# An intermediate image in HBM without zeros between its rows, and a norm factor that is zero where a shifted column has no source

## The chip, the cores and the metric

The kernel runs on one core of one Trainium2 chip. The metric is the device time in microseconds of one execution. Engines are called as the profile calls them: PE is the matmul engine (PEld its weight loads), DVE the vector engine, ACT the scalar engine, POOL the GpSimd engine, and SP the engine that issues almost all of the DMAs. Each engine runs its own list of instructions in order, and so does SP's queue of DMAs: what stands behind a waiting instruction waits too.

## The reference, cut to what matters

The input x has 32 images of 192 channels of 56 x 56 pixels. Four layers follow one another, each of the form x = x + layer(norm(x)), with a group norm over 32 groups of six channels:

```python
x = x + attention(_gn(x))          # layer 0
x = x + wkv_scan(_gn(x))           # layer 1, forwards and backwards
x = x + shift_and_smooth(_gn(x))   # layer 2
x = x + long_filter(_gn(x))        # layer 3, an FFT convolution per channel
```

The change lies around layer 2. Its 192 channels form 48 positions of four channels each; a position has an offset (dx, dy). The image of a channel is moved by the rounded offset, pixels without a source become zero, and a 3 x 3 Gaussian, whose middle is the rest of the offset, smooths what comes out:

```python
out = x[:, :, y - Ry, x - Rx] * mask      # R = round(offset), mask = source inside the image
kern = exp(-((f + delta_x)**2 + (f + delta_y)**2) / (2 * 0.5**2)); kern /= kern.sum()
out = depthwise_conv(out, kern, padding=1)
```

## The kernel before, in words

The program has four stages in a row.

`make_filter` (L250) computes layer 3's filter and its spectra: sines of a small network in chunks (`sine`, L292 to L319), a decay and a product (L324 to L337), and row and column transforms (L350 to L369). Before it computes, it issues its loads and, by `beside()`, those of attention's constants and first image (`_Ready.load`, L397). `_find_shifts` (L208), called at L282 ahead of the sines, loads the 48 offsets (L215) and computes on DVE, with one exponential on ACT, what layer 2 needs of them: the taps along x, the taps along y, the rounded dy, and in `begins` where in a row each position's read begins. Both go to HBM (L244, L247).

`attention` (L408) works image by image and writes x1 to HBM. At the end of each image, SP stores the image and its statistics (L860 to L867), and then six channels' worth of zeros (L868 to L874): x2 in HBM is laid out by channel, parity s of the image, row h (57 rows, the last one holds the mean), image pair g, and then PITCH = 112 numbers, of which the first 56 are the row and the other 56 are zeros (`gaps`, L1807 to L1810). A row read from a position shifted by up to 56 columns to either side so finds zeros where its source lies outside the image. The zeros are written from one SBUF tile, 399 KB per channel, 192 times. The order behind the last store of the image is fixed by a dependency (L873 to L874).

`scan_pairs` (L907) takes two images at a time, and `finish` (L1201) writes their rows into x2 (L1253). Its first loads (L936 to L942) stand in SP's queue behind the last image's stores.

`channel_blocks` (L1518) does layers 2 and 3 channel by channel for all 32 images at once: two images lie in 114 partitions (57 rows each), 16 pairs along the free dimension. Six channels form a group, which is also the norm's group. `prepare(c)` (L1599) is called four channels ahead. It reads the channel's image at the shifted place (L1618), 16 pieces of 56 numbers a partition, into one of three `shifted` tiles, which have a zero column at either side; POOL multiplies by the norm's factor (L1619); ACT and POOL sum the three taps along x (L1622 to L1626). `matrix(n)` (L1562) builds, once per position, the matrix of the taps along y on POOL (L1567 to L1572) and PE (L1574). `shift` (L1630) loads the channel unshifted (L1635), multiplies by that matrix (L1641) and adds (L1642). `middle`, `centre` and `spread` make layer 3's norm (L1655 to L1670). `analyse` (L1672) transforms rows (L1787) and columns (L1683) and multiplies by the filter's spectra on DVE (L1690 to L1696), `synthesise` (L1699) transforms back (L1709, L1728), adds (L1729) and stores (L1732). While the second half of one group is normed, the group before is analysed and synthesised; the main loop (L1745 to L1769) writes down one order of steps.

That order isn't the one that runs. A planner takes the instructions in program order as their priority, estimates when each will be ready, and lays down each engine's list from that; an instruction from later in the program can so stand before one from earlier. Buffers are handed out from pools of fixed counts: 15 tiles for x, eight `padded`, three `shifted`.

Of the kernel before, what the change touches and what calls it, by code (L numbers as in the profile page):

```python
# [20 lines left out]
F32 = mybir.dt.float32  # L21
I32 = mybir.dt.int32
# [6 lines left out]
C = 192  # L29
T = 96  # L30
S = 56
# [36 lines left out]

PITCH = 2 * S
# [3 lines left out]
def _resize_matrix():  # L73
# [9 lines left out]
    (114, (114,)), (114, (114,)), (114, (1,)),  # L83
# [3 lines left out]
def _constants():  # L87
# [16 lines left out]
    for t in range(2):  # L104
# [17 lines left out]
        "chan_k": _filled([f[n] for n in "f1 f2 f3 f4 ones_rows ones_u lags diff_y at_rows".split()]),  # L122
# [3 lines left out]
def _spectral_constants():  # L126
# [21 lines left out]
    for s in range(2):  # L148
# [15 lines left out]
        "diff_y": diff_y,  # L164
        "at_rows": row[:, None],
# [42 lines left out]
def _find_shifts(nc, cp, a, k, taps, begins):  # L208
# [4 lines left out]
    found = cp.tile([PR, NP, 9], F32, name="found", tag="found")  # L213
# [28 lines left out]
    for f in range(3):  # L242
        nc.vector.tensor_scalar(found[:, :, 6 + f], rnd[:, :, 1], float(1 - f), None, ALU.add)
    nc.sync.dma_start(out=taps, in_=found)  # L244
    first = cp.tile([1, NP], I32, name="first", tag="first")
# [5 lines left out]
def make_filter(ctx: ExitStack, tc: tile.TileContext, a, consts, filt, spectra, shifts, beside):  # L251
# [30 lines left out]
    _find_shifts(nc, cp, a, consts, *shifts)  # L282
# [40 lines left out]
    tc.add_manual_dep(loaded.ins, last.ins.name, behind, reason="the sines' set")  # L323
    for t in range(2):  # L324
# [83 lines left out]
def attention(ctx: ExitStack, tc: tile.TileContext, a, ready, x1, st_a, st_c, x2, gaps):  # L408

# [48 lines left out]
    zeros = cp.tile([2 * (S + 1), LEAD], F32, name="zeros", tag="zeros")  # L458
    for t in (*agents_b[0], *agents_b[1], v_a, v_c, zeros):
        nc.gpsimd.memset(t, 0.0)  # L460
    for at in (0, x2.shape[0] - LEAD):
        nc.sync.dma_start(out=x2[at : at + LEAD].unsqueeze(0), in_=zeros[0:1])
# [343 lines left out]
    for b in range(NB):  # L806
# [57 lines left out]
        for h, r in HALVES:  # L864
            stored = nc.sync.dma_start(
                out=x1[b, 128:C, 1568 * h : 1568 * h + 1568], in_=x[1][r].rearrange("p y x -> p (y x)")
            )  # L867
        for c in range(C * b // NB, C * (b + 1) // NB):  # L868
            laid = nc.sync.dma_start(
                out=gaps[c].rearrange("s h g w -> (s h) g w"),  # L870
                in_=zeros[:, 0:S].unsqueeze(1).to_broadcast([2 * (S + 1), NB // 2, S]),
            )
            behind = mybir.DependencyInfo(mybir.DependencyClass.NoSync, mybir.DependencyReason.DATA)  # L873
            tc.add_manual_dep(laid.ins, stored.ins.name, behind, reason="no burst")  # L874
# [643 lines left out]
def channel_blocks(ctx: ExitStack, tc: tile.TileContext, shifts, k, flat_x2, x2, rs2, spectra, out):  # L1518
# [12 lines left out]
    xp = ctx.enter_context(tc.tile_pool(name="d_x", bufs=15))  # L1531
# [5 lines left out]
    found = cp.tile([PR, NP, 9], F32, name="found", tag="found")  # L1537
# [11 lines left out]
    f1, f2, f3, f4, ones, ones_u, lags, diff_y, _ = pieces  # L1549
    eps = cp.tile([PR, 1], F32, name="eps", tag="eps")  # L1550
    nc.vector.memset(eps, GN_EPS)
    padded = [cp.tile([PR, NI, 64], F32, name=f"padded{i}", tag=f"padded{i}") for i in range(8)]
# [3 lines left out]
    shifted = [cp.tile([PR, NI, S + 2], F32, name=f"shifted{i}", tag=f"shifted{i}") for i in range(3)]  # L1556
# [5 lines left out]
    def matrix(n):  # L1562

        if n not in made:
            t = [wp.tile([PR, PR], F32, name=f"tap{f}", tag=f"tap{f}", bufs=1) for f in range(3)]
            for f in range(3):
                nc.gpsimd.tensor_scalar(  # L1567
                    t[f], diff_y, found[:, n, 6 + f : 7 + f], found[:, n, 3 + f : 4 + f], ALU.is_equal, ALU.mult
                )
            mat = wp.tile([PR, PR], F32, name="mat", tag="mat", bufs=3)  # L1570
            nc.gpsimd.tensor_tensor(t[0], t[0], t[1], ALU.add)
            nc.gpsimd.tensor_tensor(mat, t[0], t[2], ALU.add)  # L1572
# [24 lines left out]
    SPAN = PR * NI * PITCH  # L1597

    def prepare(c):  # L1599
# [12 lines left out]
        if c % 4 == 0:  # L1612
            begin_at[i] = nc.values_load(
                begins[0:1, i : i + 1], engines=(mybir.EngineType.SP,), min_val=LEAD - S, max_val=LEAD + S
            )
        t = shifted[c % len(shifted)]
        there = flat_x2[bass.ds(begin_at[i] + c * SPAN, SPAN)].rearrange("(p g w) -> p g w", p=PR, w=PITCH)
# [312 lines left out]
```

## Time and profile before

| what | value |
|---|---|
| runs | 12225.82, 12207.08, 12215.15 us; median 12215.15 us |
| the profiled execution | 12216.98 us, span 12215.1 us, mean granted PE clock 0.958 |
| filter, to 163 us | PE 91.0 us busy, DVE 78.6 |
| attention, 163 to about 4920 us | PE and DVE busy over 80% |
| scan, about 4920 to 8435 us | DVE busy 3013 of the 3100 us from 5200 to 8300 |
| channels, about 8435 us to the end | from 8700 to 12000: PE 3163, DVE 2953, ACT 2088, POOL 1249 of 3300 us |
| HBM | 482.13 MB read, 319.29 MB written |
| DMA packets | 1959211, of which 1821153 are under 512 bytes |

A line of a timeline gives the start, the time from the first to the last of the instructions merged in it, the engine, the line of the program, the operation, its output and inputs, and how many there were; in brackets is the idle time of the engine before it and what ended that. A line of the groups gives the count, the busy time in all and the mean of one in ns, and behind the second bar the idle time before them.

### The profile page before, as it was taken

The page shows a single profiled execution, that of the slowest core. Times are in us where ns is not written, and L with a number is a line of the kernel's source. Part 1 is how long each engine was busy: PE and PEld are TensorE (multiplying, and loading weights), DVE is VectorE, ACT ScalarE, POOL GpSimd, SP SyncE. Part 2 cuts the span into 40 slices and gives each one's busy share as a digit, 9 for nine tenths or more (in the row PEclk, how much of TensorE's full clock was granted, in tenths as well). Part 3 has the DMA queues.
Part 4 walks back from the last instruction along what each step waited for, and adds up shares of the span by engine and source line. Part 5 has one row for each costly group of instructions (what it writes and reads, how often), then busy time and mean ns, then how long its engine had stood idle before and what let it go on. Part 6 is the DMA issues. An engine that isn't in the chain of part 4 may idle for free. (4 is left out here: it accounts for less than half of the span.)

```text
span 12215.1 us, 157485 instructions
## 1 busy us (share of the span) xinstructions
PE 11030.6 (90%) x57358; PEld 6623.6 (54%) x57358; DVE 10753.1 (88%) x14722; ACT 7146.9 (59%) x14690; POOL 3400.5 (28%) x2568
## 2 busy tenths in 40 slices
PE   6999999999999999688888888886999999999999
PEld 3555555555555555333333333333666666666666
DVE  6888888888888888799999999996888899898897
ACT  3555555555555555466666666665666666666665
POOL 0000000000000000455555555555343343343330
PEclk9999999999999999899999999997999999999999
DMA  2222222222222222243334334334333333333331
GB/s 70 57 57 57 59 58 64 59 59 59 63 61 57 57 57 49 73 103 96 97 101 104 93 97 104 98 96 100 71 68 64 67 70 64 67 70 64 67 69 32
DMA packets 1959211, 876.56 MB, mean 72 GB/s; under 512 B 1821153, under 2 KB 1858292, under 8 KB 1949292
## 3 DMA queue, kind: packets, MB, share of 16 engines
q1 hardware_dynamic: 1948188, 840.69, 30.1%
q10 hardware_dynamic: 10240, 25.70, 0.8%
q8 instruction: 458, 7.50, 0.3%
q14 instruction: 325, 2.66, 0.1%
HBM read 482.13 MB, written 319.29 MB: 66 GB/s over the span
## 5 line engine op out<-in xcount | busy, mean ns | idle before, releaser
L619 DVE SCALAR_TENSOR_TENSOR o<-v_a,att_w,o 128x896 f32<-128x896 f32 (+1 forms) x1024 | 1056.8, 1032 | 467.3 <-ACT v_a L593 337.3
L1142 POOL MEMSET f<- 128x1 f32 x96 | 8.9, 99 | 4769.6 <-DMA st_c<-st 4764.6
L1793 ACT COPY y<-ps 64x252 f32<-64x252 f32 (+1 forms) x2376 | 808.7, 340 | 797.3 <-PE ps L1787 767.6
L1626 POOL TENSOR_TENSOR smooth<-smooth,more 114x896 f32<-114x896 f32 x384 | 866.3, 2259 | 1200.7 <-ACT more L1625 1141.2
L1709 PE MATMUL ps<-fixed,real 84*84 84x112 f32 x6144 | 1093.6, 260 | 0.0
L1709 PE MATMUL ps<-fixed,imag 84*84 84x112 f32 x6144 | 1091.1, 259 | 0.0
L1717 ACT ACTIVATE z<-ps,rs 84x112 f32<-84x112 f32 x3072 | 816.7, 355 | 322.1 <-PE ps L1709 319.5
L1709 PEld LDWEIGHTS ps<-fixed,real 84*84 84x84 f32 x6144 | 790.2, 154 | 158.4 <-issue 129.4
L1135 ACT ACTIVATE q<-q 128x784 f32<-128x784 f32 x384 | 328.5, 855 | 812.4 <-DVE q L1130 641.2
L1709 PEld LDWEIGHTS ps<-fixed,imag 84*84 84x84 f32 x6144 | 765.8, 153 | 0.0
L890 PE MATMUL ps<-sq,fixed 128*128 128x392 f32 x512 | 298.9, 746 | 425.9 <-ACT sq L1213 425.9
L636 ACT ACTIVATE pr<-ps,low 98x896 f32<-98x896 f32 (+1 forms) x384 | 352.3, 918 | 559.9 <-DVE low L634 559.9
L724 PE MATMUL ps<-gq_a,xs_a 128*112 128x294 f32 x1792 | 619.1, 427 | 45.7 <-DVE pq L729 45.7
L1787 PE MATMUL ps<-fixed,padded 114*128 114x168 f32 x3072 | 527.6, 322 | 134.6 <-DVE x L1729 118.3
L619 DVE SCALAR_TENSOR_TENSOR o<-v_c,att_w,o 128x448 f32<-128x448 f32 (+1 forms) x1024 | 638.3, 623 | 6.0 <-ACT v_c L604 0.9
L632 PE MATMUL ps<-xs_a,gk_a 128*98 128x448 f32 (+1 forms) x1536 | 637.1, 495 | 0.0
L633 PE MATMUL ps<-xs_c,gk_c 125*98 125x448 f32 (+1 forms) x1536 | 631.6, 492 | 0.0
L1728 PE MATMUL ps<-z,fixed 84*114 84x448 f32 x1536 | 609.7, 539 | 0.4 <-ACT z L1717 0.4
L725 PE MATMUL ps<-gq_c,xs_c 125*112 125x294 f32 x1792 | 608.3, 421 | 0.0
L890 PE MATMUL ps<-x,weights 128*128 128x392 f32 x1536 | 574.0, 517 | 31.1 <-DVE bv L1164 14.2
L737 ACT ACTIVATE pq<-pq 112x1176 f32<-112x1176 f32 x224 | 265.4, 1185 | 553.0 <-DVE pq L729 430.1
L1787 PEld LDWEIGHTS ps<-fixed,padded 114*128 114x128 f32 x3072 | 473.6, 198 | 206.1 <-DVE x L1729 140.5
(372 smaller groups left out, 29249.8 us busy)
## 6 DMA issues: line engine op xcount, KB each, us to landing
x<-x SPq DMA_DIRECT2D x576, 392.0 KB
x<-x SPq DMA_DIRECT2D x512, 196.0 KB
x<-zeros SPq DMA_DIRECT2D x192, 399.0 KB
shifted<-x SPq DMA_DIRECT2D x192, 399.0 KB
x<-x SPq DMA_DIRECT2D x192, 399.0 KB
out_x<-x SPq DMA_DIRECT2D x384, 196.0 KB
x<-in_x SPq DMA_DIRECT2D x32, 1568.0 KB
x<-x SPq DMA_DIRECT2D x32, 1568.0 KB
```

Of the source, the lines that this page charges most:

```text
L619: nc.vector.scalar_tensor_tensor(dst, tap(i), dww[:, t, i : i + 1], dst, ALU.mult, ALU.add)
L632: mm(ps[P2, h, :n], g[:, cols], xs_a[j][:, px], start=True, stop=False)
L633: mm(ps[P2, h, :n], gk_c[0:KC, 2 * j + h, cols], xs_c[j][0:KC, px], start=False, stop=True)
L724: mm(ps[:SUB, i, :HA], xs_a[j][:, px], g, start=True, stop=False)
L725: mm(ps[:SUB, i, :HA], xs_c[j][0:KC, px], gq_c[0:KC, 2 * j + (q + i) // ns], start=False, stop=True)
L890: mm(out, aa, srcs[t][h], start=True, stop=False)
L1626: nc.gpsimd.tensor_tensor(y, y, more, ALU.add)
L1709: nc.tensor.matmul(ps[:84, i * 2 * S : (i + 1) * 2 * S], part[:, i0 + i].rearrange("p s u -> p (s u)"), f3[:, m, :], start=(m == 0), stop= ...
L1717: nc.scalar.activation(z[:, i0 + i].rearrange("p m w -> p (m w)"), ps[:84, i * 2 * S : (i + 1) * 2 * S], AF.Copy, scale=q.rs[:, i0 + i : i ...
L1728: nc.tensor.matmul(got, f4[:, m, :], z[:, i0 : i0 + n, m, :], start=(m == 0), stop=(m == 1))
L1787: nc.tensor.matmul(ps[:, g * 168 : (g + 1) * 168], flat[:, (g0 + g) * 128 : (g0 + g + 1) * 128], f1, start=True, stop=True)
L1793: nc.scalar.copy(y[64 * m : 64 * m + 64, 2 * g0 + i : 2 * (g0 + n) : 2], got[64 * i : 64 * i + 64, :, :, m, :])
```

## The change

Rows of x2 now follow each other without gaps, PITCH is gone, and nothing writes zeros between them; two stores of 64 zeros, ahead of the first and behind the last row, move from attention into `_find_shifts`. The shifted read takes 896 numbers in one piece a partition, into a tile of its own (`took`, two buffers). At columns without a source this reads the end of the neighbouring row. The norm's factor is therefore made a tile of the full size, the factor times a row that is 1 where the column has a source and 0 elsewhere; it is made on POOL by two comparisons and two products once per position and group of norm (64 times in all), and POOL's product per channel is that of `took` and this tile, into one of now two `shifted` tiles. `found` carries two more numbers per position for the comparisons, and a constant holds the columns' numbers.

Beside this, `_find_shifts` is called after the sines instead of before them; the matrices of positions 0 and 1 are built on DVE; for channels 0, 2 and 4 DVE multiplies and adds the second and third tap in one instruction each, in place of ACT's product and POOL's sum; x has 14 buffers instead of 15, `padded` seven instead of eight.

```diff
@@ _find_shifts
+    for f in range(2):
+        nc.vector.tensor_scalar(found[:, :, 9 + f], rnd[:, :, 0], f * S - 0.5, None, ALU.add)
     nc.sync.dma_start(out=taps, in_=found)
+    zeros = cp.tile([1, LEAD], F32, name="zeros", tag="zeros")
+    nc.vector.memset(zeros, 0.0)
+    for at in (0, x2.shape[0] - LEAD):
+        nc.sync.dma_start(out=x2[at : at + LEAD].unsqueeze(0), in_=zeros)
@@ make_filter
     beside()
-    _find_shifts(nc, cp, a, consts, *shifts)
...
     tc.add_manual_dep(loaded.ins, last.ins.name, behind, reason="the sines' set")
+    _find_shifts(nc, cp, a, consts, *shifts)
@@ attention
-        for c in range(C * b // NB, C * (b + 1) // NB):
-            laid = nc.sync.dma_start(
-                out=gaps[c].rearrange("s h g w -> (s h) g w"),
-                in_=zeros[:, 0:S].unsqueeze(1).to_broadcast([2 * (S + 1), NB // 2, S]),
-            )
...
@@ channel_blocks
-    xp = ctx.enter_context(tc.tile_pool(name="d_x", bufs=15))
+    xp = ctx.enter_context(tc.tile_pool(name="d_x", bufs=14))
...
-    padded = [cp.tile([PR, NI, 64], F32, name=f"padded{i}", tag=f"padded{i}") for i in range(8)]
+    padded = [cp.tile([PR, NI, 64], F32, name=f"padded{i}", tag=f"padded{i}") for i in range(7)]
...
-    shifted = [cp.tile([PR, NI, S + 2], F32, name=f"shifted{i}", tag=f"shifted{i}") for i in range(3)]
+    shifted = [cp.tile([PR, NI, S + 2], F32, name=f"shifted{i}", tag=f"shifted{i}") for i in range(2)]
@@ matrix
+            engine = nc.vector if n < 2 else nc.gpsimd
...
-            nc.gpsimd.tensor_tensor(t[0], t[0], t[1], ALU.add)
-            nc.gpsimd.tensor_tensor(mat, t[0], t[2], ALU.add)
+            engine.tensor_tensor(t[0], t[0], t[1], ALU.add)
+            engine.tensor_tensor(mat, t[0], t[2], ALU.add)
@@ prepare
+        if (n, i) not in factors:
+            here, low = (wp.tile([PR, S], F32, name=m, tag=m) for m in ("here", "low"))
+            nc.gpsimd.tensor_scalar(here, at_cols, found[:, i, 9:10], None, ALU.is_gt)
+            nc.gpsimd.tensor_scalar(low, at_cols, found[:, i, 10:11], None, ALU.is_lt)
+            nc.gpsimd.tensor_tensor(here, here, low, ALU.mult)
+            factor = wp.tile([PR, NI, S], F32, name="factor", tag="factor")
+            nc.gpsimd.tensor_tensor(
+                factor, _bc(scales[n][:, j], [PR, NI, S]), here.unsqueeze(1).to_broadcast([PR, NI, S]), ALU.mult
+            )
...
+        took = wp.tile([PR, NI, S], F32, name="took", tag="took")
+        there = flat_x2[bass.ds(begin_at[i] + c * SPAN, SPAN)].rearrange("(p g w) -> p g w", p=PR, w=S)
+        nc.sync.dma_start(out=took, in_=there)
         t = shifted[c % len(shifted)]
-        there = flat_x2[bass.ds(begin_at[i] + c * SPAN, SPAN)].rearrange("(p g w) -> p g w", p=PR, w=PITCH)
-        nc.sync.dma_start(out=t[:, :, 1 : S + 1], in_=there[:, :, 0:S])
-        nc.gpsimd.tensor_tensor(t, t, _bc(scales[n][:, j], [PR, NI, S + 2]), ALU.mult)
+        nc.gpsimd.tensor_tensor(t[:, :, 1 : S + 1], took, factors[n, i], ALU.mult)
...
         for f in (1, 2):
+            if c < GROUP and c % 2 == 0:
+                nc.vector.scalar_tensor_tensor(y, t[:, :, f : f + S], taps[f], y, ALU.mult, ALU.add)
+                continue
             more = wp.tile([PR, NI, S], F32, name="more", tag="spare", bufs=3)
             nc.scalar.activation(more, t[:, :, f : f + S], AF.Copy, scale=taps[f])
             nc.gpsimd.tensor_tensor(y, y, more, ALU.add)
```

## The prediction

> **What bounds the kernel now.** I read the busy shares and slices first, then the windows by stage, then the waits and the chain around each seam that the edit touches.
>
> ```profile
> PE 11030.6 (90%) x57358; PEld 6623.6 (54%) x57358; DVE 10753.1 (88%) x14722; ACT 7146.9 (59%) x14690; POOL 3400.5 (28%) x2568
> ...
> PE   6999999999999999688888888886999999999999
> DVE  6888888888888888799999999996888899898897
> POOL 0000000000000000455555555555343343343330
> ```
>
> Four stages: filter (to 163 us), attention (to 4920), scan (to 8435), channels (to the end). No engine waits for a DMA inside attention, and in the scan ACT waits 15.1 us in all for x. The edit's places are three seams and the channel stage. The first seam, attention to scan, is SP's queue by time (start, us):
>
> ```profile
> 4926.92 1.23 SPq L865 DMA_DIRECT2D x<-x  x2
> 4928.19 30.03 SPq L869 DMA_DIRECT2D x<-zeros  x6
> 4958.33 5.58 SPq L936 DMA_DIRECT2D passing<-in_scan_o  x1
> 4963.96 0.42 SPq L936 DMA_DIRECT2D passing<-in_scan_c  x1
> ```
>
> The scan's first weights queue behind the last image's six zero stores; the waits give PE 44.3 us idle there, on "DMA x<-zeros". Nothing else runs.
>
> The second seam is inside the filter, DVE by time; the third, POOL at the entry to the channels:
>
> ```profile
> 56.82 0.21 DVE L218 TENSOR_SCALAR off<-off 114x96 f32<-114x96 f32 x1 [19.07 <-DMA off<-in_L_conv_offset]
> ```
> ```profile
> 8458.03 1.74 POOL L1619 TENSOR_TENSOR shifted<-shifted,scale 114x928 f32<-114x928 f32 x1
> ...
> 8475.54 8.42 POOL L1626 TENSOR_TENSOR smooth<-smooth,more 114x896 f32<-114x896 f32 x4
> ```
>
> The chain runs through POOL from 8450 to 8581. In the steady part the groups of lines from 8700 to 12000 are what I price with (mean ns of one, then idle before):
>
> ```profile
> L1626 POOL TENSOR_TENSOR smooth<-smooth,more 114x896 f32<-114x896 f32 x344 | 779.1, 2268 | 1152.2 <-ACT more L1625 1107.3 <-ACT smooth L1622 31.8
> L1619 POOL TENSOR_TENSOR shifted<-shifted,scale 114x928 f32<-114x928 f32 x170 | 310.4, 1826 | 443.9 <-DMA shifted<-x 443.8
> L1567 POOL TENSOR_SCALAR tap<-fixed,found 114x114 f32<-114x114 f32 x116 | 119.0, 1031 | 6.8
> ```
>
> Last, windows from one group's mean (L1657) to the next: length, PE, PEld, DVE, ACT, POOL busy, granted clock:
>
> ```profile
> 10104.10:10220.77 116.67, 111.85 (x653) 78.80 (x653) 103.85 (x154) 73.22 (x196) 46.57 (x28) 0.97 0.31 66
> 10220.77:10334.41 113.64, 108.34 (x651) 76.64 (x651) 102.91 (x152) 72.19 (x194) 41.53 (x23) 1.00 0.31 67
> 11940.91:12054.66 113.75, 110.16 (x651) 78.47 (x651) 99.89 (x153) 66.91 (x189) 26.84 (x12) 0.97 0.18 38
> ```
>
> PE is busy 94 to 96% of a group, DVE about 90%: PE sets the pace, DVE is close behind it. The 27 groups from 8607 to 11710 have a mean of 114.9 us: 14 with one tap matrix 114.1 (POOL 41.8), 13 with two 115.8 (POOL 46.6).
>
> **The change part by part.** The sum is against the profiled execution's 12216.98 us (span 12215.1); the median of the runs, 12215.15, lies 1.8 lower.
>
> *Zero stores gone (192 of 399 KB).* The last six take 30.03 us of SP's queue with every engine idle. The first load behind them takes 5.58 us to issue where its neighbour takes 0.42, so the seam gives 30.0 to 35.2 us. Late next are the weights' landing and the st_a round trip, which moved behind too. I take **-33**, between the ends, as x1's last store is still in flight at 4928. The other 186 stores lie in attention, where SP itself waits 2358 us for ACT at L566 and no engine waits for a DMA: nothing. Were SP late there, 30 us an image would already show as a wait.
>
> *x2 without gaps.* The scan writes as many 224-byte pieces, 224 bytes apart instead of 448: nothing, under DVE's 97% there; were the stores slower, ACT's 15.1 us of waiting for x might double (+15). In the channels two reads a channel become 114 long pieces instead of 1824. In steady flow only POOL waits for one: 129 waits, 444 us. The read took 6.08 us in the chain at 9253.8. Long pieces have one near row: found and fixed (800 KB) issued at 8444.6 and read at 8450.3. So 399 KB takes from 3 us (half of it) to 6.1 (no better).
>
> *One buffer fewer* of x, padded, shifted. A load of x goes out one channel (19 us) later; nobody waits for x now, and it is used four or more steps after its buffer frees. The sixth padded waits for PE's L1787 of the fifth instead of the fourth channel of the group before, a step (19 us) earlier than it: nothing. Without that cover, some 2 us of DVE a group (+60). The read goes to its own tile, so SP's L1618 no longer waits for ACT (532 us), only for POOL's product two channels back; out_x stores are queued behind it and gain.
>
> *_find_shifts later.* DVE stands 19.07 us at L218 for a 43 KB load that SP issues after the loads of attention. In program order its 22 DVE instructions now follow the sines; its loads keep their place in SP's queue. But the planner places by readiness: L326 and L332, from after the sines, already run between them (11.21, 17.50), and L218 sits in a gap of the sines. A lower priority moves it by one instruction while its load is thought to come when it did. Two new TENSOR_SCALARs and a memset (0.2 us each) and two zero stores, which move to SP's queue here from the start of attention, have slack behind taps. Bounds -19 and +1; I take **0**.
>
> *Entry to the channels.* POOL loses matrices 0 and 1 (each 3 x 0.757 + 2 x 0.426 = 3.1) and six adds of channels 0, 2, 4 (6 x 2.08): 18.7 us. It gains, up to channel 5, two factors of 3.1 (two TENSOR_SCALARs of 114x56 at half of 0.757 and a little, a small product at 0.3, a large one at 2.07) and six products at 2.08 instead of 1.74 (two full inputs, as L1626): 8.2 us. DVE, idle over 80% there, takes the adds at 1.15 (L619's form at 128x896) and the matrices. So channel 5, at which group 0 closes (8510), comes 10.5 us earlier. But group 1 needs channels 6 to 11, with another 8.2 added and nothing removed: -2.3 by the sum alone. Of POOL's 28 us of idling from 8444 to 8580, 14.2 are waits for ACT's products, half of which go with DVE's adds. Ends -25 and 0; I take **-12**.
>
> *Steady part.* POOL per group of six: products 6 x (2.27 - 1.83) = 2.6, two factors at 3.5 with today's contention: 9.6 us on 44. POOL's own idling covers that. The price is on DVE: L1692 (84x420) takes 0.58 us alone, 0.81 in the mean and 2.0 beside a POOL instruction; L1696 0.98, L1661 1.32 against 1.07; L1690 and L1643, with one input from PSUM or only one, never stretch. Summed over 172 channels that is some 350 us of stretch now.
> For the time I have two rows. A second matrix adds 4.8 us of POOL and 1.67 us of period; without its own PE (0.36) and DVE (0.26) time 1.05, so 0.22 us per us of POOL: 9.6 x 0.22 x 31 = +65. The last group, with 15 us less POOL, is only 0.36 shorter than a one-matrix group: 0.02, +6. Below nothing: the seven groups with a full clock take 113.2, 1.7 under the mean, -53 if all did. I take 0.1, **+28**: the matrix row is the nearer in kind, but the change also frees POOL from its waits for DMA, so that part of the work can lie in the half of a group where PE alone sets the pace.
>
> The Trainium skill (GPSIMD Engine Reference, section 8, Key points) speaks against this change: GpSimd shares its SBUF interfaces with VectorE and contends with DVE instructions that have two SBUF inputs. The rows agree on which instructions stretch; a sum by the rule alone, every extra POOL microsecond exposed, would be 9.6 x 31 = +298, against the +28 from the rows. The same page (section 4.1, Engine selection) has one-input GpSimd work at roughly line rate; here L1567 with one tensor input takes 0.757 us where a two-input product of its size takes 0.426, so the small steps of a factor would cost less by the page (an estimate: 0.3 us less each) and the steady term +23.
>
> Sum: -33 + 0 - 12 + 28 = -17, 12200 on the profiled execution, **12198** as a median. What a measurement of this kernel can tell from no change is about 0.2%, 24 us.
>
> **The rivals.**
> - *The filter's wait goes too* (-19): the planner puts L218 behind the last sine. For it: 22 instructions lose their precedence. Against: L332 fills the same gaps today. 12179.
> - *POOL against DVE decides* (slower): the stretch sits in the half of a group that holds the centres, where DVE is the chain. For it: two-matrix groups end at clocks of 0.97 to 0.99, PE cooling after a wait for DVE x L1729 (114 us in all). At slope 0.22, +65 and 12235; if every group takes the slowest one's 118.2, +101 and 12271; between them, 12253. It cancels the gains from 45 / 31 = 1.45 us a group, and is slower by over 0.2% from 2.2. Against: the last group's row.
> - *Steady part faster*: POOL without waits for DMA (3.4 us each) relieves ACT's order, and more groups run like the seven at 113.2: up to -53, 12117. Against: PE waits only 10.8 us for ACT rs in all.
> - *The read isn't one piece after all*: packets of the channel stage stay; the entry then gives -7, inside the first case.
>
> **How the numbers follow.** First case 0.36 (own range 12165 to 12225; faster 0.14, same 0.22); filter 0.24 (faster 0.19, same 0.05); slower 0.28 (slower 0.21, same 0.07); steady gain 0.12 (faster). Faster 0.45, same 0.34, slower 0.21. The range cuts the far half of the steady gain and the slower case past its middle: 12130 to 12255.
>
> **What would show it.** Attention to scan: L936 straight behind L865, PE's idle 11 us. Filter: the wait before L218. Entry: the first L1641 comes 14 us, group 0's L1657 10 us sooner after SP's first load. Steady: POOL 54 us a group, L1692's and L1696's mean up by a fifth, period 115.8; no POOL wait on the read. Wrong if the planner orders the group anew, so that the period leaves 113 to 118.

## The result, and the profile after

The changed kernel takes **12571.02 us** (median of 6 runs, 12569.26 to 12573.27) against 12214.14 us before (6 runs, 12207.08 to 12225.82): a ratio of **1.0291, 95% interval 1.0278 to 1.0305**, 357 us slower. The prediction was 12198 us, range 12130 to 12255. The profiled execution took 12569.26 us, its span is 12567.3.

The page of the changed kernel: busy time, three of the rows of slices, and the chain that ended last by engine.

```profile
PE 11211.5 (89%) x57358; PEld 6746.2 (54%) x57358; DVE 10896.8 (87%) x14741; ACT 7142.6 (57%) x14684; POOL 3662.4 (29%) x2805
...
PE   7999999999999998888888888868898898988889
...
DVE  6888888888888887999999999968888888888887
...
PE 15%; POOL 8%; ACT 5%; DVE 4%; issue 1%; DMA 0%; SPq 0%; DVEq 0%; POOLq 0%; ACTq 0%
```

POOL has 262 us more work. PE is busy 181 us longer and DVE 144 us longer with nearly the same instructions, ACT as long as before. In the channels PE falls from nines to eights, and the chain, which ran through PE and DVE before (POOL 2%, ACT 1%), now runs through POOL and ACT for 13% of the span.

The stages show where the time went. Every milestone is a line of both traces (us from the start):

| up to | before | after | difference of this part |
|---|---|---|---|
| first image's statistics stored | 349.52 | 347.21 | -2.3 |
| last image's statistics stored | 4923.86 | 4880.43 | -41.1 |
| scan's weights issued | 4964.43 | 4887.72 | -33.3 |
| channels' load of `found` issued | 8444.64 | 8366.57 | -1.4 |
| group 0's mean | 8517.65 | 8433.18 | -6.4 |
| last group's mean | 12054.66 | 12406.88 | **+436.7** |
| end | 12215.1 | 12567.3 | 0 |

So the changed kernel is 84 us ahead when the steady part of the channels begins, and there it loses 437. The seam is as it was foretold; in SP's queue by time the scan's first load now follows the last store:

```profile
4883.48 1.23 SPq L867 DMA_DIRECT2D x<-x  x2
4885.00 1.02 SPq L929 DMA_DIRECT2D passing<-in_scan_o  x1
...
4887.72 0.48 SPq L934 DMA_DIRECT2D weights<-in_scan_w  x1
```

In the filter, DVE's wait for the offsets is where it was:

```profile
57.35 0.21 DVE L218 TENSOR_SCALAR off<-off 114x96 f32<-114x96 f32 x1 [19.32 <-DMA off<-in_L_conv_offset]
```

The windows from mean to mean of three groups in the middle (length, then PE, PEld, DVE, ACT, POOL busy, granted clock, DMA share, GB/s):

```profile
9828.08:9957.57 129.49, 116.39 (x651) 81.62 (x651) 108.18 (x153) 72.25 (x194) 57.06 (x35) 0.93 0.22 58
9957.57:10087.49 129.92, 116.63 (x653) 81.48 (x653) 106.61 (x153) 73.14 (x196) 52.32 (x32) 0.93 0.22 59
...
12288.80:12406.88 118.08, 111.20 (x651) 78.89 (x651) 103.48 (x152) 67.81 (x190) 30.24 (x13) 0.97 0.15 37
```

27 groups have a mean of 129.57 us (before: 114.91), nearly all of them 129.5 or 129.9; this mean of the same 27 groups is called the period below. The last group, which prepares nothing, takes 118.08. POOL does 10.6 us more a group than before, the period grows by 14.7, and PE sits idle 13 us a group where it was idle 5: it loses time by waiting (and its granted clock falls to 0.93, from between 0.97 and 1.00). What is waited for, the waits from 8700 to 12300 us say (total, times, longest):

```profile
DVE x L1652 <- PE ps L1651: 411.1, 209, 6.9
ACT smooth L1629 <- POOL shifted L1626: 248.4, 54, 4.6
...
PE ps L1797 <- ACT rs L1679: 128.2, 28, 4.6
PE ps L1738 <- ACT z L1727: 123.8, 55, 3.7
```

In the kernel before, from 8700 to 12000 us, PE hardly waited for ACT's `rs` and `z`:

```profile
PE ps L1787 <- ACT rs L1669: 10.8, 13, 1.2
...
PE ps L1728 <- ACT z L1717: 0.4, 2, 0.2
```

The second line of the changed kernel is new: ACT's first tap now waits for POOL's product, twice a group. The timeline of all engines at such a place (start, length, engine):

```profile
9835.99 4.86 POOL L1636 TENSOR_TENSOR smooth<-smooth,more 114x896 f32<-114x896 f32 x2 [8.14 <-ACT more L1635]
...
9840.81 2.52 POOL L1626 TENSOR_TENSOR shifted<-took,factor 114x896 f32<-114x896 f32 x1
...
9843.37 1.04 ACT L1629 ACTIVATE smooth<-shifted,found 114x896 f32<-114x896 f32 x1 [4.61 <-POOL shifted L1626]
...
9844.32 4.21 ACT L1803 COPY y<-ps 64x252 f32<-64x252 f32 x12
...
9845.84 0.94 PE L1693 MATMUL re<-y,fixed 128*84 128x420 f32 x2 [1.79 <-ACT y L1803]
```

POOL sums two taps of one channel, then multiplies the next; ACT's first tap stands and waits for that, and behind it in ACT's list stand the twelve row copies y of the analysis, for which PE waits. The copies need nothing of the tap: only ACT's list joins them. The other first tap that waits stands in the same way among the copies `z`. At the end of the half of a group that holds the centres, two later taps wait for POOL's sums, and behind them stands `rs`, which closes the norm. They stand ahead of it in the kernel before too; what is new there is that POOL is so late:

```profile
9884.25 1.04 ACT L1635 ACTIVATE more<-shifted,found 114x896 f32<-114x896 f32 x1 [2.04 <-POOL smooth L1636]
9889.20 1.04 ACT L1635 ACTIVATE more<-shifted,found 114x896 f32<-114x896 f32 x1 [3.91 <-POOL smooth L1636]
9890.15 0.25 ACT L1679 ACTIVATE rs<-ps,eps 84x16 f32<-84x16 f32 x1
```

In the kernel before, ACT's list has the copies at the place of the first tap, then two squares and two later taps, and this tap behind them; its waits hold none of a first tap for POOL. ACT by time there:

```profile
10118.67 4.24 ACT L1793 COPY y<-ps 64x252 f32<-64x252 f32 x12 [3.45 <-PE ps L1787]
10122.94 1.79 ACT L1663 ACTIVATE sq<-padded 114x896 f32<-114x896 f32 x2
...
10128.53 1.06 ACT L1622 ACTIVATE smooth<-shifted,found 114x896 f32<-114x896 f32 x1
```

The orders of PE's and DVE's lists in the middle groups are the same in both kernels.

### The profile page after: what moved, and what is told of

It is laid out like the page before. It is cut to its first block, busy times and chain, and to the rows that moved or that the text cites. A ratio compares the mean times of both kernels' runs of the same rounds, so it can differ in the third digit from the quotient of the medians.

```text
span 12567.3 us, 157336 instructions
## 1 busy us (share of the span) xinstructions
PE 11211.5 (89%) x57358; PEld 6746.2 (54%) x57358; DVE 10896.8 (87%) x14741; ACT 7142.6 (57%) x14684; POOL 3662.4 (29%) x2805
## 5 line engine op out<-in xcount | busy, mean ns | idle before, releaser
L1738 PE MATMUL ps<-z,fixed 84*114 84x448 f32 x1536 | 669.7, 574 | 137.0 <-ACT z L1727 137.0
L1797 PE MATMUL ps<-fixed,padded 114*128 114x168 f32 x3072 | 595.7, 352 | 174.1 <-ACT rs L1679 131.8
L1797 PEld LDWEIGHTS ps<-fixed,padded 114*128 114x128 f32 x3072 | 547.6, 224 | 247.3 <-ACT rs L1679 139.7
L1706 DVE TENSOR_TENSOR imag<-a,a 84x420 f32<-84x420 f32 (+1 forms) x576 | 635.4, 1103 | 4.2
L1652 DVE TENSOR_TENSOR x<-x,ps 114x448 f32<-114x448 f32 x384 | 236.5, 619 | 457.5 <-PE ps L1651 442.9
```

The costliest lines, as they stand in the source:

```text
L1706: nc.vector.tensor_tensor(to[1], a0, a1, ALU.add)
L1738: nc.tensor.matmul(got, f4[:, m, :], z[:, i0 : i0 + n, m, :], start=(m == 0), stop=(m == 1))
L1797: nc.tensor.matmul(ps[:, g * 168 : (g + 1) * 168], flat[:, (g0 + g) * 128 : (g0 + g + 1) * 128], f1, start=True, stop=True)
```

## The experiments

Six parts of the change meet in the steady part: POOL's work for the mask, two shifted tiles, seven padded, 14 tiles of x, the packed reads, and the read's own tile. A wait between lists can also come from the planner's order alone. Runs 1 to 9, 13 and 14 have one execution each. The kernel before, on the same chips, took 12216.57 us beside runs 1 to 4 and 12226.17 beside runs 5 to 8 (one execution each), 12216.48 beside runs 9 to 12 (median of 20, from 12202.9 to 12237.4) and 12217.8 beside runs 13 to 15 (median of 7).

**1. _find_shifts early again.**

```diff
+    _find_shifts(nc, cp, a, consts, *shifts)      # ahead of the sines
-    _find_shifts(nc, cp, a, consts, *shifts)      # behind them
```

> The changed kernel with _find_shifts called before the sines again, nothing else; it computes all. The planner, which lays the lists down anew, then gives the channel stage's ACT another repeating order: the changed kernel's has one first tap (L1629) in the middle of the z copies of the half of a group that holds the centres, this one has it one step earlier, while all buffers and all work per group stay. Theory A (the order of ACT's list costs the steady part its 14.7 us a group): the period falls from 129.6 to about 115, the time to about 12571 - 31 x 14.7 = 12115 us. Theory B (POOL's added work, 10 us a group, decides): period 129, 12571. Theory C (two shifted tiles lock POOL and ACT together): 129, 12571. Theory D (seven padded): 129, 12571.

12584.07 us, period 129.66. The premise fell: in the trace the lists of ACT and POOL in a group are those of the changed kernel, so this run tells nothing of theory A. It says that the place of `_find_shifts` has no part in the loss. The run is 13 us slower than the changed kernel: attention's last statistics are stored 7 us later here, `found` is loaded 10.5 us later. One execution doesn't show that the place does this, for in run 7, whose edit does not touch attention, the last statistics come 11.7 us later than in the kernel before.

**2. Three shifted tiles.**

```diff
-    shifted = [... for i in range(2)]
+    shifted = [... for i in range(3)]
-            factor = wp.tile([PR, NI, S], F32, name="factor", tag="factor")
+            factor = wp.tile([PR, NI, S], F32, name="factor", tag="factor", bufs=1)
```

> The changed kernel with three shifted tiles instead of two (and one factor tile instead of two, to make room); it computes all. ACT's list comes out the same as in the run with _find_shifts early. Theory C: POOL's product runs a channel ahead again, no first tap waits for it, period 115, 12115 us. Theory A: about 115 too, but then the run with two tiles and the same order is as fast. Theories B and D: period 129, 12571.

12426.2 us, period 124.75: 145 us of the loss, neither all nor nothing. With three tiles one of the two taps that wait has gone further back, the other still stands ahead of the copies, so the run changes the tiles and the place of a tap together. The waits from 8700 to 12000 us:

```profile
PE ps L1797 <- DVE x L1739: 223.3, 93, 5.5
...
ACT smooth L1629 <- POOL shifted L1626: 120.0, 26, 4.6
```

**3. No mask.**

```diff
-        if (n, i) not in factors: ... factor ...
-        nc.gpsimd.tensor_tensor(t[:, :, 1 : S + 1], took, factors[n, i], ALU.mult)
+        nc.gpsimd.tensor_tensor(t[:, :, 1 : S + 1], took, _bc(scales[n][:, j], [PR, NI, S]), ALU.mult)
```

> The changed kernel without the factor tile: POOL multiplies the read by the broadcast factor as before, and the columns without a source are not set to zero, so this part of the computation is left out. POOL does some 12 us less a group; ACT's list is in the order of the changed kernel. Theory B: period back to 115 or less, about 12115 us. Theories A and C: the waits stay, only the products on the chain are 0.7 us shorter, six a group: period 125 to 127, 12430 to 12490. Theory D: 129.

12363.86 us, period 123.28: 207 us. POOL has 43.0 and 46.8 us a group again, as before the change, and still the period is 8.4 us longer than before. POOL's work by itself isn't all of it.

**4. Eight padded tiles.**

```diff
-    padded = [... for i in range(7)]
+    padded = [... for i in range(8)]
```

> The changed kernel with eight padded tiles instead of seven (and one factor tile instead of two, to make room); it computes all. The lists of ACT and POOL keep the changed kernel's order. Theory D (the sixth centre waits for the row transform of the group before): period back to 115, 12115 us. Theories A, B and C: period 129.6, 12571.

12572.15 us, period 129.69: nothing. Theory D is out, and the single factor tile, which the run also has, is worth nothing.

**5. No mask and three shifted tiles**, the edits of 3 and 2 together.

> The changed kernel without the factor tile (columns without a source are not set to zero: that part of the computation is left out) and with three shifted tiles. The two edits gave 207 us (no mask) and 145 us (three shifted) one by one, of some 455 us that the steady part lost. Theory E (both causes are separate and add up): 12571 - 207 - 145 = 12219 us, period 118. Theory F (either removes the same lock-step between POOL and ACT): about 12364, period 123. If the two are all of it and more than additive: period 115, 12116.

12221.12 us, period 118.35: theory E to 2 us. The two add up (143 us for the third tile here, 145 in run 2), and 3.4 us a group are left that neither explains.

**6. The kernel before with the mask's work.**

```diff
+        if (n, i) not in factors: ... factor ...       # as in the change, bufs=1
-        nc.gpsimd.tensor_tensor(t, t, _bc(scales[n][:, j], [PR, NI, S + 2]), ALU.mult)
+        nc.gpsimd.tensor_tensor(t[:, :, 1 : S + 1], t[:, :, 1 : S + 1], factors[n, i], ALU.mult)
```

> The kernel before with POOL's new work alone: factor tile, comparisons and the product of two full inputs, on the gapped x2, read in place into three shifted tiles (seven padded to make room, shown to be worth nothing). ACT's list keeps the order of the kernel before. Theory B (POOL's work by itself): period 114.9 + 6.7 = 121.6, 12215 + 207 = 12422 us. Theory G (POOL's work costs only where ACT's list has first taps ahead of the row copies y, as in the changed kernel): period 115 to 117, 12215 to 12280.

12305.39 us, 79 over the kernel before in its series, period 117.57, with ACT's list in the order of the kernel before. Between the two theories: the same work that costs 207 us in the changed kernel costs well under half of it here, but not nothing.

**7. The kernel before with two shifted tiles.**

```diff
-    shifted = [... for i in range(3)]
+    shifted = [... for i in range(2)]
```

> The kernel before with two shifted tiles instead of three, nothing else. The read then waits for ACT's third tap two channels back, and the planner's list changes a little. Theory C (two tiles lock POOL and ACT together in any case): period 114.9 + 4.7 = 119.6 or more, 12360 us or more. Theory G (it is the order of ACT's list in the changed kernel): 12215, period 115 to 116.

12279.57 us, 53 over, period 116.75: again between, and a third of what the tile is worth in the changed kernel. The run is no clean test of the tile: the planner laid the lists of ACT, PE and DVE anew, and attention, which the edit does not touch, ends 12 us later than in the kernel before. Both edits are dearer in the changed kernel, by a factor of nearly three. One thing that is common to them there is the order; run 9 tests it.

**8. The zero stores back**, into a tensor that nothing reads.

```diff
+        for c in range(C * b // NB, C * (b + 1) // NB):
+            laid = nc.sync.dma_start(out=spare[c]..., in_=zeros[:, 0:S]...)
```

> The changed kernel with the 192 zero stores in attention again, of the same shape and place in SP's queue, into a tensor that nothing reads. The lists of PE and ACT stay those of the changed kernel. If the stores cost what the traces of the two kernels differ by up to the channels' first load (78 us: 43 up to the last store of x1, 33 at the seam), 12571 + 76 = 12647 us. If attention's 43 us come from another place of the change, only the seam's 33 come back: 12604.

12644.59 us, +73.6 where 76 were expected. The last image's statistics are stored at 4921.76 us again (changed kernel 4880.43), the weights are issued at 4962.31. The stores cost attention at least as much as the seam. Every kernel with them in SP's queue (the one before and runs 6, 7 and 8) stores the last statistics between 4921.8 and 4935.6 us, every kernel without them between 4875.5 and 4887.5. How, DVE's waits in attention show; first the changed kernel, from 163 to 4870 us:

```profile
DVE o L621 <- ACT v_a L595: 292.6, 66, 5.9
```

Then this run, same window:

```profile
DVE o L622 <- ACT v_a L596: 337.3, 95, 5.9
```

The kernel before has the same 337.3 us. Without the stores DVE waits 45 us less for ACT, twice an image instead of three times: in its list three statistics of the next image's x (BATCH_NORM_STATS2 `st_a<-x`) now stand among the sums that wait for ACT, and fill the gap. With the stores in SP's queue the planner has them behind those sums. PE's and ACT's lists in attention are the same in this run and in the changed kernel.

**9. No mask, three tiles, read in place.**

```diff
-        took = wp.tile([PR, NI, S], F32, name="took", tag="took")
-        nc.sync.dma_start(out=took, in_=there)
-        nc.gpsimd.tensor_tensor(t[:, :, 1 : S + 1], took, _bc(scales[n][:, j], [PR, NI, S]), ALU.mult)
+        nc.sync.dma_start(out=t[:, :, 1 : S + 1], in_=there)
+        nc.gpsimd.tensor_tensor(t, t, _bc(scales[n][:, j], [PR, NI, S + 2]), ALU.mult)
```

> As the run without the mask and with three shifted tiles (12221 us, period 118.3), but the read goes straight into the shifted tile again and POOL multiplies there, as before the change; x2 stays without gaps. Columns without a source are not set to zero. ACT's list is then in the order of the kernel before: the row copies y ahead of the first tap, not behind it. Theory H (what is left of the loss comes from the tile of its own for the read, because the planner then takes POOL's product for early and puts a first tap that waits for it ahead of the row copies): period 114.9, 12221 - 31 x 3.4 = 12115 us. Theory I (it comes from something else in the channel stage, such as the 14 tiles of x or the packed transfers): 12221.

12115.01 us, theory H to the microsecond, which is closer than two executions of a kernel agree; period 114.81, as in the kernel before. So the read's own tile was the third cause, and 14 tiles of x and the packed transfers cost the period nothing.

**10. The changed kernel with the read in place and three tiles.**

```diff
-        took = wp.tile(...); nc.sync.dma_start(out=took, in_=there)
-        nc.gpsimd.tensor_tensor(t[:, :, 1 : S + 1], took, factors[n, i], ALU.mult)
+        nc.sync.dma_start(out=t[:, :, 1 : S + 1], in_=there)
+        nc.gpsimd.tensor_tensor(t[:, :, 1 : S + 1], t[:, :, 1 : S + 1], factors[n, i], ALU.mult)
```

> The changed kernel, all computed, with the read in place into three shifted tiles (one factor tile's buffers are kept at two). What is left of the change in the steady part is POOL's work for the mask, with ACT's list in the order of the kernel before. From the run of the kernel before with the mask (12305 us) less what the stores cost (74) and 10 to 15 us of the entry: 12215 to 12225, period 117.6. If the mask costs 6.7 us a group whatever the order: 12115 + 207 = 12322.

**12169.36 us** (5 runs; ratio to the kernel before 0.9962, 95% interval 0.9948 to 0.9976): faster than before, with everything computed, and 402 us faster than the change as it was written. It is also 46 us under the lower of the two expectations, which took the mask's price from run 6. Period 116.15. ACT by time at the place shown above: the copies stand first, and the tap waits for nothing.

```profile
10051.09 4.24 ACT L1802 COPY y<-ps 64x252 f32<-64x252 f32 x12 [3.44 <-PE ps L1796]
10055.35 1.91 ACT L1672 ACTIVATE sq<-padded 114x896 f32<-114x896 f32 x2
...
10061.06 1.06 ACT L1628 ACTIVATE smooth<-shifted,found 114x896 f32<-114x896 f32 x1
```

Against run 9 the mask costs 54 us in all, and in the groups 1.35 us for 8.3 us more on POOL, a slope of 0.16. In run 6 the same 8.3 us of POOL lengthened the groups by 2.66 us, a slope of 0.32, with ACT's list in the same order; what makes it dearer there is open. Two groups of this kernel's windows:

```profile
10036.52:10152.53 116.01, 110.66 (x653) 77.86 (x653) 103.69 (x154) 73.28 (x196) 53.35 (x36) 0.99 0.28 67
10152.53:10267.37 114.84, 110.24 (x651) 77.87 (x651) 103.15 (x153) 71.96 (x194) 51.02 (x31) 0.99 0.27 66
```

**11. Zero stores from POOL's queue**, in the kernel before, laid over the first 31 images.

```diff
-        for c in range(C * b // NB, C * (b + 1) // NB):
-            laid = nc.sync.dma_start(
+        for c in range(C * b // (NB - 1), min(C, C * (b + 1) // (NB - 1))):
+            laid = nc.gpsimd.dma_start(
```

> The kernel before, all computed, with its zero stores issued by POOL's queue instead of SP's and laid out over the first 31 images. POOL, which has nothing else to do in attention, issues all of them early. DVE's list in attention comes out with the statistics of x ahead of the sums that wait for ACT, as in the changed kernel. If it was the stores' time in SP's queue that cost (theory S): both the seam's 31 and attention's 43 us are gained, 12216 - 74 = 12142 us. If it was their traffic (theory T): attention slows down or stays, at most the seam is gained, 12185 or more.

12223.05 us (10 runs; ratio 1.0005, 0.9995 to 1.0014): no change. That lies in theory T's range and outside theory S's, but each has its share. POOL issues all 192 by 1455 us. In these first images one takes 150 to 163 us, where it takes 146.7 in the changed kernel and 147.5 to 149.2 in the kernel before; from then on the times are the changed kernel's, and so is the order of DVE's list. The seam's 31 us and the later images' gain are there; the burst eats them. PE from 200 to 1400 us waits for a load that has none of these waits before:

```profile
PE ps L633 <- DMA gk_c<-once: 48.5, 8, 10.8
```

**12. The same, with the change's work at the entry.**

```diff
+            engine = nc.vector if n < 2 else nc.gpsimd        # matrix()
...
+            if c < GROUP and c % 2 == 0: nc.vector.scalar_tensor_tensor(...)
...
+    _find_shifts(nc, cp, a, consts, *shifts)                  # behind the sines
```

> The zero stores from POOL's queue, and from the change also _find_shifts behind the sines, the two first matrices on DVE, and the taps of channels 0, 2 and 4 on DVE; x2 keeps its gaps, the read and the factor stay as before, all is computed. The entry to the channels was 9 us sooner in the changed kernel than in the one before, the later _find_shifts gave 2 to 13 us: 12142 - 10 to 20 = 12122 to 12132 us. If these parts are worth nothing without the rest of the change: 12142.

12204.47 us (10 runs, from 12177 to 12245; 0.9992, 0.9980 to 1.0005): 19 us under run 11, the upper end of what was expected for these parts, but the spread is as wide. The expected time rested on a gain that run 11 did not bring. The interval of the ratio includes 1.

**13. One first tap moved.** Run 2 with a fixed order of one instruction a group (`done` holds each channel's third tap; the dependency orders ACT's list alone).

```diff
+        if c % GROUP == 4 and c - 2 in done:      # the first tap of c stays behind the third tap of c - 2
+            tc.add_manual_dep(first.ins, done[c - 2].ins.name, behind, ...)
```

> The changed kernel with three shifted tiles (12426 us, period 124.7), the read still in a tile of its own, all computed; one first tap a group (channel 4 of six) is held behind the last third tap of two channels before. ACT's list is then, instruction for instruction of the channel stage's groups, in the order of the kernel before; POOL's list stays that of the run with three shifted tiles. Theory J (the place of this one tap in ACT's list is the cost of the read's own tile): the row copies no longer wait, period 116 as with the read in place, 12426 - 31 x 8.6 = 12160 us. Theory K (POOL's order, or something else about the tile of its own, costs it): 12400 to 12426.

12284.09 us, period 119.81: 142 of the 257 us that lie between runs 2 and 10. Neither theory alone: the place of this one tap is a little over half of the read's own tile. ACT's wait for POOL's product is gone from the list of waits. What is left goes with DVE; the windows of two groups, to be read against those of run 10:

```profile
9010.69:9129.36 118.67, 110.28 (x651) 77.62 (x651) 106.76 (x152) 72.27 (x194) 52.62 (x31) 0.99 0.24 64
9129.36:9249.57 120.21, 111.35 (x653) 78.60 (x653) 107.20 (x154) 73.20 (x196) 56.12 (x36) 0.97 0.24 64
```

DVE is busy 3.1 us a group more than in run 10 (mean of 27 groups) with the same instructions in the same order, and PE waits 211 us for DVE's `x` where it waited 114. POOL's product takes longer too: 2497 ns in the mean, 2027 in run 10, where it reads in place. POOL's list in this run is that of run 2. That POOL's order makes DVE's and POOL's instructions longer fits these numbers, and so does something about the tile itself; no run moved POOL's order alone, so it stays open.

**14. The tap moved with two tiles**, in the changed kernel.

```diff
+        if c % GROUP == 3 and c - 1 in done:      # the first tap of c stays behind the third tap of c - 1
+            tc.add_manual_dep(first.ins, done[c - 1].ins.name, behind, ...)
```

> The changed kernel itself with two shifted tiles, all computed; the first tap of channel 3 of six is held behind the last third tap of channel 2, so that it stands behind the row copies and the two squares instead of ahead of them. Another first tap stays between the z copies behind it. Theory J: of the 257 us that the place of the tap cost with three tiles most come back, 12571 - 200 to 260: 12310 to 12370 us, and the rest of the loss is that the other first tap waits for one of two tiles. Theory L (with two tiles POOL's product cannot start until ACT has read the tile, wherever the taps stand): 12500 to 12571.

12472.75 us, period 126.25: 98 us, half of what theory J wanted and more than theory L allowed. PE still waits 83 us for `rs` and 135 for `z`, which stand behind taps that wait for POOL. With two tiles the order and the lock-step both cost.

**15. The zero stores paced, from POOL's queue**, with the parts of run 12. The tile that the stores read is written from each image's statistics times zero, so that POOL waits for the image.

```diff
+        zero = zeroes[b % 2]
+        nc.gpsimd.tensor_scalar(zero[:, 0:9], st[: 2 * (S + 1), 0], 0.0, None, ALU.mult)
...
-            laid = nc.sync.dma_start(out=gaps[c]..., in_=zeros[:, 0:S]...)
+            nc.gpsimd.dma_start(out=gaps[c]..., in_=zero[:, 0:S]...)
```

> The kernel before with the zero stores issued by POOL's queue, now six at the end of each of the first 31 images (the tile that they read is written anew from the image's statistics times zero), with the later _find_shifts and the entry's work on DVE; all is computed. Before, all stores early slowed nine images by some 9 us each, PE waiting for the load of gk_c behind them. Theory S (it is the stores' place in SP's queue and in the planner's list, not their traffic): 12216 - 74 - 10 to 19 = 12123 to 12132 us. Theory T (their traffic costs what they cost anywhere): 12200.

**12138.6 us** (4 runs; ratio 0.9932, 95% interval 0.9916 to 0.9949): the fastest kernel of the study that computes everything, 7 us above theory S's range and far from theory T. All 77 MB of zeros are still written, and attention runs like the changed kernel's, an image in 145.9 to 149.2 us. DVE's list in attention is in the changed kernel's order, with its wait (from 163 to 4870 us):

```profile
DVE o L620 <- ACT v_a L594: 292.4, 65, 5.9
```

So it was not the traffic that set that order, but the queue. In SP's queue the scan's load follows the last store:

```profile
4884.32 1.24 SPq L866 DMA_DIRECT2D x<-x  x2
4885.86 0.99 SPq L937 DMA_DIRECT2D passing<-in_scan_o  x1
```

The runs as one sum from the kernel before to the changed one, each term a difference of two runs: 12214 less 74 (zero stores, run 8), less 25 (what is left: 12115 + 74 against 12214; in run 9's trace 16 of it lie ahead of group 0's mean, the rest behind it), plus 54 (mask, runs 10 and 9), plus 257 (own tile for the read, runs 2 and 10), plus 145 (two tiles, run 2) is 12571. Such a sum closes by itself; it says how the loss divides, each term to the 10 or 20 us by which single executions differ. The size of a term depends on the order in which they are taken: without the mask the own tile costs 106 (runs 5 and 9), not 257.

## Why the prediction was wrong

- **Zero stores gone, -33.** At the seam this is what came: -33.3 us between the last statistics and the scan's weights, PE's wait there 10.5 us instead of 44.3 (foretold: 11). But "the other 186 stores lie in attention ... nothing" failed, by 41 us. That no engine waits for a DMA was true and proved too little: the stores' cost was not a wait for their data but their place in SP's queue, with which the planner laid DVE's list less well (runs 8 and 15).
- **x2 without gaps, nothing.** Right: the scan is 1.4 us shorter, and run 9 has the old period with packed reads. POOL no longer waits for the read, as foretold.
- **One buffer fewer, nothing.** Right for `padded` (run 4) and x (run 9). For `shifted` it was wrong: the prediction dealt with the read's wait and not with POOL's product, which with two tiles cannot start before ACT has read the product of two channels back three times. 145 us in run 2, the tap that its new order moved included.
- **_find_shifts later, 0.** The wait at L218 stayed, as foretold, and the rival that it would go did not come. The first image ends 2.3 us sooner and run 1 took 13 us more, but the first image ends between 343.9 and 352.5 us in the four kernels with the early call and between 342.2 and 348.5 in the eleven with the later one (runs 11 and 12, with their burst of stores, left aside). A gain of a few us may be there; none is shown.
- **Entry, -12.** Right in sign, half in size: -6.4 us to group 0's mean, the first product of `shift` 8.6 us sooner (foretold 10 and 14).
- **Steady part, +28.** This is the step that failed: +437. Its own mechanism, POOL's work against DVE, was a small part of that. POOL does 10.6 us more a group (foretold 9.6), and the mask's part of it cost 54 us with the old order (run 10), at a slope of 0.16, and 79 in run 6, at 0.32, where 0.1 was taken and 0.22 was the far row. (By its own factors, 0.1 x 9.6 x 31, the term is 30, not 28.) Both two-input products of DVE were to grow by a fifth; from 8700 us on `imag` went from 892 to 1134 ns in the mean and `real` from 918 down to 847. What was missing is that "the read goes to its own tile" was booked as a gain: "SP's L1618 no longer waits for ACT". The planner then put a first tap ahead of the row copies, and on the chip POOL's product was not done by then: up to 4.6 us, once or twice a group, with PE's work behind it. That the order goes with the tile is shown (runs 5 and 9 differ in the tile alone); that the planner reckoned with an earlier product is our reading of it. The tile cost 257 us with the mask, 106 without. Of the 257, 142 are shown to be the place of one tap (run 13); how the rest comes about is open.
- **The rivals.** "POOL against DVE decides" was on the right side, with +65 to +101 for the steady part about a fifth of what came, and by another road: PE's waits for what stands behind ACT's waits for POOL are the larger part, 11 us a group in the changed kernel, and its wait for DVE's `x` is 2. That it was on the right side is luck. The sentence that named the way to be wrong was the last one, "if the planner orders the group anew, so that the period leaves 113 to 118". It had no chance and no price, though the prediction itself said that the planner places by readiness, and the edit moved the readiness of a tile that every channel passes through.
- **The rule of the Trainium skill** (GPSIMD Engine Reference, section 8, Key points): GpSimd contends with DVE instructions that have two SBUF inputs. By the rule alone, every microsecond exposed, the mask would have cost 298 us; runs 9 and 10 show 54, with DVE's `padded` at 1377 ns in the mean instead of 1301, `imag` at 918 instead of 869, and `real` unchanged at 924. The instructions that grew are among those that the rule names; the price is not in it. Where POOL's work falls may set it, as run 13 against run 10 suggests; no run shows that.

## What to carry to other kernels

When a planner lays down the lists, an edit that makes an input ready sooner can be an edit of the order on every engine that uses it; ask which instruction will now stand first in an in-order list, whether what it waits for will truly be there, and who stands behind it. A buffer's count is to be checked against all its users, the slowest reader above all, and not only against the transfer that fills it. Work that no engine waits for can still cost through its place in a queue: look at what the planner does with that place, and try the same work on a queue that is idle, at the same pace.

## What the runs showed of the hardware

- A store of 399 KB in 1824 pieces took SP's queue 5.0 us (30.03 for six at the seam) and POOL's 2.04 us; from POOL it landed 19.4 us after its issue in the median (run 11). 192 of them issued as fast as POOL can took the DMA engines' busy share from 0.25 to 0.74 and made PE wait for a load on SP's queue by up to 10.8 us; six at the end of each image left the images as long as without them (runs 11 and 15).
- POOL's product of two full inputs (114x896) took 2.50 us in the mean in the changed kernel, where it reads a tile of its own, and 2.03 in run 10, where it reads in place; the one with a broadcast factor 2.11 (run 3) and 1.83 (the kernel before, 114x928). So the second full input cost POOL 0.2 to 0.4 us here and the tile of its own 0.3 to 0.5, the way the products then fall beside DVE's work included.
- A small instruction can be stretched much: the first comparison of 114x56 in the changed kernel (`here`) took 0.41 us at least, 0.96 in the mean, and 2.06 where it started beside DVE's `padded`. The second (`low`), of the same size, took 0.44 in the mean.
- PE's granted clock was lower where PE waited more: 0.93 in the changed kernel's groups of 129.5 us, of which PE is idle 13, and 0.97 to 1.00 in groups of 114.8 (run 9), idle about 5. Idle time alone does not order the runs: it is 11.4 us a group in run 2 at 0.96 and 10.5 in run 14 at 0.93. Part of the longer period is this: PE's 651 matmuls of a group are busy 116.4 us in the changed kernel and 108.3 to 110.0 in run 9.
